# Transformer block on one core: attention scores from exactly split q and k in three one-pass products, and P V after every two key tiles

## The chip, the cores and the metric

The kernel runs on one core of a Trainium2 chip. The metric is the device time of one execution in microseconds, as the median over runs. All work of an engine is queued in the order in which the program issues it: TensorE (PE, with its weight loads PEld), VectorE (DVE), ScalarE (ACT), GpSimd (POOL), and SyncE (SP), which here issues all the DMAs.

## The reference

One pre-norm block on x of 2 x 2048 x 256 in float32: attention with a compressed key/value (rank 64) and a compressed query (rank 128), 16 heads, then a gated feed-forward part with weights given as whole numbers. A head's q and k have 48 numbers: 16 of content and 32 with rotary position (rope). Cut to what matters here:

```python
q = jnp.concatenate([q_content, q_rope], axis=-1)      # (2, 16, 2048, 16 + 32)
k = jnp.concatenate([k_content, k_rope], axis=-1)
scores = jnp.einsum('bhqd,bhkd->bhqk', q, k) * scale
scores = jnp.where(causal[None, None], scores, -inf)
attn = jax.nn.softmax(scores, axis=-1)
out = jnp.einsum('bhqk,bhkd->bhqd', attn, v)
x = x + out.transpose(0, 2, 1, 3).reshape(Bx, Tx, 256) @ W_o
x = x + ffn(layernorm(x))
```

## The kernel before

**First stage.** The sequence is cut into chunks of 512 tokens, four for each batch, eight in all. For each chunk the kernel normalizes, transposes and projects, applies rope, and stores q and k, head by head and transposed, in DRAM (`qr`, `kr` for the rope rows, `qc_d`, `kc` for the content rows). V stays in SBUF. From the fifth chunk on, `load_first` puts the first pieces of the attention stage between the projections: four k loads, two q loads, two empty places, and `from_first` for the first step.

**Attention.** A step is a batch b, a group u of four heads and a chunk g of 512 queries; there are 32, with g running fastest. It goes over the key chunks c = 0 to g. A key chunk has four key tiles of 128; in the last one (c = g, the diagonal chunk) tile j has only the queries from 128 j on, so products are 512, 384, 256 and 128 wide. Four heads stand as two pairs r and two row halves a: the 48 rows of a head lie at partitions 0 to 47 or 64 to 111, so two heads' products (one for each half) use different rows of the PE array. For each key tile and pair r, `scores` makes two float32 products into one PSUM tile of two banks (three such tiles, `ps_big`), ACT takes exp of both banks at once into an `es` tile (12 of them), and in the diagonal chunk POOL clears what lies above the diagonal. `values` multiplies by V: four heads use 32 columns of the array each and add into one PSUM tile `acc`. At the end of a step `gather` copies `acc` (ACT) and stores it (`ad`).

The order is written out by hand and kept for all five engines. All four tiles of a key chunk are scored, then the first tile of the next chunk, and only then comes P V of the finished chunk:

```python
for k, job in enumerate(jobs):
    job()
    if k == 0 and waiting:
        waiting.pop()()
    if c == 0 and k == 1 and i + 1 < len(steps):
        from_first(*steps[i + 1])
```

`load_q` brings a step's q two steps ahead, `load_k` its k four steps ahead, each with four DMAs (two of rope rows, two of content rows). `from_first` (L142) subtracts the first key from all keys, which changes no softmax.

**Other work in the attention stage.** `loads` also stores V, loads and converts the feed-forward weights, and for the first batch's chunks calls in turn `packed` (gathers a chunk's attention output and sums), `inverted` (1/sum, sent round through DRAM into `rb`) and `divided`. Near the end, `early` starts the output projection and layer norm of the first two chunks.

**Feed-forward part.** Its matmuls already work on fp32r halves ("hi" and "lo") of their inputs: `gu` (L722) and `d` (L750).

Of the kernel before, what the change touches and what calls it, by code (L numbers as in the profile page):

```python
# [30 lines left out]
AHEAD = 2  # L31
LN_EPS = 1e-5
RMS_EPS = 1e-6
NEG = -3.0e38
# [6 lines left out]
def block_kernel(ctx: ExitStack, tc: tile.TileContext, x, w_kv, g_kv, w_kc, w_v, w_q, w_qh, w_kr, w_o,  # L41
# [14 lines left out]
    qpool = qkv.enter_context(tc.tile_pool(name="qpool", side="right", bufs=AHEAD + 1))  # L56

    ident = const.tile([P, P], FP, tag="ident", name="ident")
    make_identity(nc, ident)
# [64 lines left out]
    kT, qT = {}, {}  # L124
    k_tiles = [kpool.tile([P, 2, CH], FP, tag=f"kT_{i}", name=f"kT_{i}") for i in range(2 * NC)]
    k0 = {}

    def load_k(b, u, g):
        kT[b, u, g] = t = k_tiles[u % 2 * NC + g]
        load_heads(t, kr[b, g], kc[b, g][:, :HD, :], u)  # L130

    def from_first(b, u, g):


        t = kT[b, u, g]
        if g == 0:
            k0[b, u] = small.tile([P, 2], FP, tag="k0", name=f"k0_{b}_{u}")
        for a in range(2):
            rows = slice(64 * a, 64 * a + DIM)
            if g == 0:  # L140
                nc.vector.tensor_copy(k0[b, u][rows], t[rows, :, 0])
            nc.vector.tensor_tensor(t[rows], t[rows], k0[b, u][rows].unsqueeze(2).to_broadcast([DIM, 2, CH]),  # L142
                                    ALU.subtract)

    def load_q(b, u, g):
        qT[b, u, g] = t = qpool.tile([P, 2, CH], FP, tag="qT", name=f"qT_{b}_{u}_{g}")
        load_heads(t, qr[b, g], qc_d[b, g], u)

    written = ExitStack()

# [1 line left out]
    with ExitStack() as actx:  # L152
# [204 lines left out]
        def job(i, k):  # L357
            if i < len(chunks):
                chains[i][k]()
# [21 lines left out]
        for d in range(2):  # L381
            rope_columns(w_kr_sb[:, d, :], w_kr_raw[d])

        first_loads = ([(load_k, step) for step in steps[:NC]] + [(load_q, step) for step in steps[:AHEAD]]
                       + 2 * [(lambda *step: None, steps[0])] + [(from_first, steps[0])])

        def load_first(i):
            if i >= NC and first_loads:
# [3 lines left out]
        for i, one in enumerate(chunks):  # L392
# [35 lines left out]
            if i == 0:  # L428
                for to in kc.values():
                    nc.sync.dma_start(out=to[:, HD, :], in_=ones)  # L430

    fw = ctx.enter_context(tc.tile_pool(name="fw", bufs=1))
    apool = ctx.enter_context(tc.tile_pool(name="apool", bufs=4))
# [24 lines left out]
    def inverted(b, g):  # L458

        n = f"{b}_{g}"  # L460
        rec = small.tile([P, 64], FP, tag="rec", name=f"rec_{n}")
        nc.vector.reciprocal(rec, parts_of[b, g])  # L462
        rd = dram.tile([NH, CH], FP, tag="rd", bufs=4, name=f"rd_{n}")
        nc.sync.dma_start(out=rd.rearrange("h (j i) -> (h j) i", i=64), in_=rec)
        parts_of[b, g] = rb = apool.tile([P, 2, CH], FP, tag="rb", bufs=2, name=f"rb_{n}")
# [65 lines left out]


    with ExitStack() as actx:
        espool = actx.enter_context(tc.tile_pool(name="espool", side="right", bufs=12))
# [5 lines left out]
        def exp_jobs(b, u, g):  # L540

            n = f"{b}_{u}_{g}"
            es = {}
            last_kt = NT * (g + 1) - 1

            def first(kt):
                c, j = divmod(kt, NT)
                return c, j, j * P if c == g else 0

            def scores(kt, p):  # L550

                c, j, off = first(kt)
                pairs = (0, 1) if off >= CH // 2 else (p,)

                def job():
                    if p not in pairs[:1]:
                        return
                    w = CH - off
                    ps = big(f"st_{n}_{kt}_{p}")
                    e = espool.tile([P, 2, CH], FP, tag="es", name=f"es_{n}_{kt}_{p}")  # L560
                    for i, r in enumerate(pairs):
                        for a in range(2):
                            rows = slice(64 * a, 64 * a + DIM)
                            nc.tensor.matmul(ps[:, a, i * w:(i + 1) * w],  # L564
                                             lhsT=kT[b, u, c][rows, r, j * P:(j + 1) * P],
                                             rhs=qT[b, u, g][rows, r, off:], start=True, stop=True)
                        es[kt, r] = e[:, :, i * w:(i + 1) * w]
                    used = len(pairs) * w
                    nc.scalar.activation(e[:, :, :used], ps[:, :, :used], AF.Exp, scale=SCALE)  # L569
                    if c == g:  # L570
                        if len(pairs) == 1:
                            block, pattern = e[:, :, :P], [[0, 2], [1, P]]
                        else:
                            block = e[:, :, :used].rearrange("k a (r q) -> k a r q", r=2)[:, :, :, :P]
                            pattern = [[0, 2], [0, 2], [1, P]]
                        nc.gpsimd.affine_select(out=block, in_=block, compare_op=ALU.is_ge, fill=0.0, base=0,  # L576
                                                pattern=pattern, channel_multiplier=-1)
                return job

            def values(*kts):  # L580
                def job():
                    if kts[0] == 0:
                        acc[b, u, g] = ps_acc.tile([P, CH], FP, tag="acc", name=f"acc_{n}")
                    for kt in kts:
                        c, j, off = first(kt)
                        for p in range(2):
                            for a in range(2):
                                h = 4 * u + 2 * p + a
                                r0 = 32 * (2 * p + a)
                                nc.tensor.matmul(acc[b, u, g][r0:r0 + 32, off:],  # L590
                                                 lhsT=vv[b, c][:, j, h * VW:h * VW + 32],
                                                 rhs=es[kt, p][:, a], start=(kt == 0), stop=(kt == last_kt),
                                                 tile_position=(0, r0))
                return job

            def gather():
                at = fin.tile([P, CH], FP, tag="at", name=f"at_{n}")
                nc.scalar.copy(at, acc[b, u, g])  # L598
                nc.sync.dma_start(out=ad[b, g][4 * u:4 * u + 4].rearrange("h e f -> (h e) f"), in_=at)

            jobs = []
            for c in range(g + 1):
                kts = range(c * NT, (c + 1) * NT)
                job = values(*kts)
                if c == g:
                    job = lambda job=job: (job(), gather())
                jobs.append(([(lambda kt=kt: (scores(kt, 0)(), scores(kt, 1)())) for kt in kts], job))
            return jobs

        def loads(i):  # L610

            if i + AHEAD < len(steps):
                load_q(*steps[i + AHEAD])
            if i + NC < len(steps):
                load_k(*steps[i + NC])
            if i == NU * NC + 6:
                x1[0, 0] = load_x(xpool, 0, 0)
                x1[0, 1] = load_x(spare, 0, 1)
# [2 lines left out]
                nc.sync.dma_start(out=vd[one], in_=vv[one])  # L621

            j, k = divmod(i - (NU * NC + 2), 3)
            if 0 <= j < 3 or (j, k) == (3, 0):
# [7 lines left out]
        def whole(src, shape, name, n):  # L632
# [16 lines left out]
            for i in range(2):  # L649
# [15 lines left out]
        waiting = []  # L665
        for i, step in enumerate(steps):
            loads(i)
            by_chunk = exp_jobs(*step)
            for c, (jobs, values) in enumerate(by_chunk):
                for k, job in enumerate(jobs):  # L670
                    job()
                    if k == 0 and waiting:
                        waiting.pop()()
                    if c == 0 and k == 1 and i + 1 < len(steps):
                        from_first(*steps[i + 1])
                    if k in (0, 2):
                        for one, g in early.get((i, c, k), ()):
                            one(*groups[g])
                waiting.append(values)
        waiting.pop()()  # L680

    qkv.close()

# [308 lines left out]
```

## Time and profile before

| | |
|---|---|
| median of 3 runs | 1084.23 us (1083.06 to 1085.67) |
| the profiled execution | 1085.72 us, span 1083.9 us |
| granted TensorE clock | 0.997 |
| PE, ACT, DVE, POOL busy over the span | 98%, 60%, 29%, 26% |
| scores L564: matmul records, busy | 2560, 495.6 us |
| P V L590: matmul records, busy | 2560, 251.5 us |
| exp L569: instructions, busy | 576, 512.9 us |
| first stage, attention, feed-forward | to about 167 us, to about 915 us, to the end |

Busy times of matmuls include the time in which results drain, and matmuls overlap, so the step from one matmul's start to the next one's says more than its duration. A program's float32 product appears as two matmul records and two weight loads. The chain of work that ended last names, for each stretch of time, the engine that the end of the span depended on.

### The profile page before, as it was taken

The page shows a single profiled execution, that of the slowest core. Times are in us where ns is not written, and L with a number is a line of the kernel's source. Part 1 is how long each engine was busy: PE and PEld are TensorE (multiplying, and loading weights), DVE is VectorE, ACT ScalarE, POOL GpSimd, SP SyncE. Part 2 cuts the span into 40 slices and gives each one's busy share as a digit, 9 for nine tenths or more (in the row PEclk, how much of TensorE's full clock was granted, in tenths as well). Part 3 has the DMA queues.
Part 4 walks back from the last instruction along what each step waited for, and adds up shares of the span by engine and source line. Part 5 has one row for each costly group of instructions (what it writes and reads, how often), then busy time and mean ns, then how long its engine had stood idle before and what let it go on. Part 6 is the DMA issues. An engine that isn't in the chain of part 4 may idle for free.

```text
span 1083.9 us, 16862 instructions
## 1 busy us (share of the span) xinstructions
PE 1066.2 (98%) x6687; PEld 536.8 (50%) x6687; DVE 309.8 (29%) x454; ACT 653.9 (60%) x817; POOL 282.0 (26%) x379
## 2 busy tenths in 40 slices
PE   8899999999999999999999999999999999999997
PEld 5455554444443443434344344443435344889886
DVE  5577776000310220230001212004001210556552
ACT  3243336777776776777777767767766766343242
POOL 4566756002110200211111021021101111445353
PEclk9999999999999999999999999999999999999999
DMA  7746746112410421311131133132201000342201
GB/s 180 238 162 216 251 162 201 40 40 78 135 61 1 145 68 61 94 54 40 37 103 39 31 99 99 40 81 79 60 5 45 11 10 20 126 124 63 80 20 43
DMA packets 54457, 93.27 MB, mean 86 GB/s; under 512 B 9312, under 2 KB 23008, under 8 KB 54368
## 3 DMA queue, kind: packets, MB, share of 16 engines
q1 hardware_dynamic: 54368, 92.09, 27.6%
q8 instruction: 55, 0.90, 0.4%
q14 instruction: 34, 0.28, 0.1%
HBM read 49.09 MB, written 42.98 MB: 85 GB/s over the span
## 4 chain that ended last, share of the span: by engine, by line
PE 82%; DVE 1%; POOL 0%; ACT 0%; issue 0%; DVEq 0%; ACTq 0%
PE st L564 45%; PE acc L590 22%; PE gu L722 8%; PE d L750 4%; PE ps_o L485 3%; PE tp_f L528 1%; POOL es L576 0%; DVE h L729 0%; DVE small_ones L696 0%; DVE x_f_lo L530 0%; POOL rstd_f L69 0%; POOL rstd_f L70 0%; ACT es L569 0%; ACT x_f_hi L529 0%; DVE y L757 0%
## 5 line engine op out<-in xcount | busy, mean ns | idle before, releaser
L569 ACT ACTIVATE es<-st 128x1024 f32<-128x1024 f32 (+1 forms) x576 | 512.9, 993 | 170.0 <-PE st L564 168.2
L564 PE MATMUL st<-qT,kT 48*128 48x512 f32 (+3 forms) x2560 | 495.6, 536 | 1.7 <-ACT v_sb L348 1.2
L564 PEld LDWEIGHTS st<-qT,kT 48*128 48x128 f32 x2560 | 226.0, 186 | 250.8 <-ACT es L569 119.7
L576 POOL TENSOR_SCALAR_AFFINE_SELECT es<-es 128x256 f32<-128x256 f32 (+1 forms) x192 | 97.4, 516 | 641.1 <-ACT es L569 641.1
L590 PE MATMUL acc<-es,v_sb 128*32 128x512 f32 (+3 forms) x2560 | 251.5, 531 | 0.7 <-POOL es L576 0.7
L590 PEld LDWEIGHTS acc<-es,v_sb 128*32 128x32 f32 x2560 | 74.6, 109 | 185.4 <-issue 145.9
L142 DVE TENSOR_TENSOR kT<-kT,k 48x1024 f32<-48x1024 f32 x64 | 82.4, 1287 | 20.7 <-DMA kT<-kc 18.2
L725 ACT ACTIVATE silu<-gu 128x512 f32<-128x512 f32 x48 | 28.6, 599 | 92.9 <-PE gu L722 92.9
L734 POOL TENSOR_TENSOR hT_lo<-h,hT_hi 128x512 fp32r<-128x512 f32 x48 | 61.8, 1289 | 81.8 <-ACT hT_hi L733 74.7
L304 PE MATMUL rp_k<-xln,w_kr_sb 128*128 128x512 f32 x128 | 58.1, 598 | 0.0
L729 DVE SCALAR_TENSOR_TENSOR h<-gu,silu 128x512 f32<-128x512 f32 x48 | 33.0, 690 | 77.9 <-ACT silu L725 51.2
L462 DVE RECIPROCAL rec<-all_sums 128x64 f32<-128x64 f32 x8 | 4.4, 548 | 160.4 <-DMA all_sums<-ad 160.4
L750 PE MATMUL d<-w_d,hT_lo 128*128 128x256 f32 x192 | 46.4, 283 | 0.0
L750 PE MATMUL d<-w_d,hT_hi 128*128 128x256 f32 x192 | 46.4, 283 | 0.0
L598 ACT COPY at<-acc 128x512 f32<-128x512 f32 x32 | 18.8, 586 | 40.5 <-PE acc L590 38.1
L722 PE MATMUL gu<-x_f_hi,w_g 128*128 128x512 f32 x96 | 39.4, 411 | 0.2 <-DVE h L729 0.2
L491 DVE TENSOR_TENSOR x<-ps_o,x 128x1024 f32<-128x1024 f32 x8 | 9.8, 1225 | 101.2 <-PE ps_o L485 99.7
L722 PE MATMUL gu<-x_f_lo,w_g 128*128 128x512 f32 x96 | 37.5, 391 | 0.0
L722 PE MATMUL gu<-x_f_lo,w_u 128*128 128x512 f32 x96 | 37.4, 390 | 0.0
L722 PE MATMUL gu<-x_f_hi,w_u 128*128 128x512 f32 x96 | 37.4, 390 | 0.0
L750 PEld LDWEIGHTS d<-w_d,hT_lo 128*128 128x128 f32 x192 | 36.8, 192 | 0.3
L750 PEld LDWEIGHTS d<-w_d,hT_hi 128*128 128x128 f32 x192 | 36.8, 192 | 0.3
(99 smaller groups left out, 764.7 us busy)
## 6 DMA issues: line engine op xcount, KB each, us to landing
kr<-tcos_k SPq DMA_DIRECT2D x16, 512.0 KB
qr<-tcos_q SPq DMA_DIRECT2D x16, 512.0 KB
kT<-kr SPq DMA_DIRECT2D x64, 128.0 KB
qT<-qr SPq DMA_DIRECT2D x64, 128.0 KB
ad<-at SPq DMA_DIRECT2D x32, 256.0 KB
x<-in_x_dram SPq DMA_DIRECT2D x15, 512.0 KB
vd<-v_sb SPq DMA_DIRECT2D x8, 574.0 KB
qc<-cont_q SPq DMA_DIRECT2D x8, 512.0 KB
```

The source lines that it names most:

```text
L142: nc.vector.tensor_tensor(t[rows], t[rows], k0[b, u][rows].unsqueeze(2).to_broadcast([DIM, 2, CH]), ALU.subtract)
L304: nc.tensor.matmul(ps[:, s, :], lhsT=w_kr_sb[:, d, cols], rhs=xln[b, g][:, d, :], start=(d == 0), stop=(d == 1))
L485: nc.tensor.matmul(ps[:, t * C:(t + 1) * C], lhsT=attn[b, g][:, d, t * P:(t + 1) * P], rhs=w_o_sb[:, d, :], start=(d == 0), stop=(d == 1))
L564: nc.tensor.matmul(ps[:, a, i * w:(i + 1) * w], lhsT=kT[b, u, c][rows, r, j * P:(j + 1) * P], rhs=qT[b, u, g][rows, r, off:], start=True, ...
L569: nc.scalar.activation(e[:, :, :used], ps[:, :, :used], AF.Exp, scale=SCALE)
L576: nc.gpsimd.affine_select(out=block, in_=block, compare_op=ALU.is_ge, fill=0.0, base=0, pattern=pattern, channel_multiplier=-1)
L590: nc.tensor.matmul(acc[b, u, g][r0:r0 + 32, off:], lhsT=vv[b, c][:, j, h * VW:h * VW + 32], rhs=es[kt, p][:, a], start=(kt == 0), stop=(kt ...
L722: nc.tensor.matmul(ps[:, k, :], lhsT=w[:, d, cols], rhs=x2[b, g][s][:, d, :], start=(d == 0 and s == 0), stop=(d == 1 and s == 1))
L725: nc.scalar.activation(s, ps[:, 0, :], AF.Silu, scale=WS)
L729: nc.vector.scalar_tensor_tensor(h, ps[:, 1, :], WS, s, ALU.mult, ALU.mult)
L734: nc.gpsimd.tensor_tensor(lo, h, hi.bitcast(FP), ALU.subtract)
L750: nc.tensor.matmul(ps[t], lhsT=parts[b, g][s][:, f, t * P:(t + 1) * P], rhs=w_d[:, f, :], start=(f == 0 and s == 0), stop=(f == NF - 1 and ...
```

## The change

- **Split.** k (after the first key is subtracted) and q are split into a high part, rounded to fp32r, and the rest. k has four copies of a head's content and two of its rope rows in 64 rows; the constant `lows` marks the rows in which the low part is to stand. `split_k` and `split_q` do this on DVE, through a shared tile `rest`.
- **Three products.** Each score group adds three fp32r products with 64 rows into the same PSUM tile: rope rows (both parts of k) with q's low part, rope rows with q's high part, and content rows (all four combinations).
- **Loads.** k is loaded in 12 DMAs (four rope, eight content) and q likewise, both two steps ahead; there are five k sets and three q sets. A table `plan` says after which key tile each load and split is issued.
- **Order.** Outside the diagonal chunk P V is issued for two key tiles at a time, two tiles later. The diagonal chunk's P V still comes after the next step's first tile; the copy of `acc` now comes one tile after that.
- **Buffers.** es 12 to 8, `attn` 4 to 3, `rb` 2 to 1; `packed(0, 3)` moves from step 27 to step 30.
- **First loads.** `load_first` now issues k and q of the first two steps and the four splits of the first step.

```diff
-    def from_first(b, u, g):
-        t = kT[b, u, g]
...
-            nc.vector.tensor_tensor(t[rows], t[rows], k0[b, u][rows].unsqueeze(2).to_broadcast([DIM, 2, CH]),
-                                    ALU.subtract)
+    def load_rope(t, ropes, u):
+        src = ropes[4 * u:4 * u + 4].rearrange("(p a) r s f -> a (r s) p f", a=2)
+        for a in range(2):
+            for i in range(2):
+                nc.sync.dma_start(out=t[64 * a + RD * i:64 * a + RD * i + RD], in_=src[a])
+    def load_content(t, contents, u):
+        src = contents[4 * u:4 * u + 4, :HD, :].rearrange("(p a) r f -> a r p f", a=2)
+        for a in range(2):
+            for i in range(4):
+                nc.sync.dma_start(out=t[64 * a + HD * i:64 * a + HD * i + HD], in_=src[a])
...
+    def split_k(b, u, g, i):
+        t = k_of(b, u, g)[i]
...
+        firsts = k0[b, u, i]
+        for p in range(2):
+            nc.vector.tensor_scalar(rest[:, p], t[:, p], firsts[:, p:p + 1], lows[:, i:i + 1], ALU.subtract, ALU.mult)
+        for p in range(2):
+            nc.vector.scalar_tensor_tensor(t[:, p].bitcast(FR), t[:, p], firsts[:, p:p + 1], rest[:, p].bitcast(FP),
+                                           ALU.subtract, ALU.subtract)
+    def split_q(b, u, g, i):
+        t, other, content = q_of(b, u, g)
+        if i:
+            nc.vector.tensor_scalar(rest, content, lows[:, 2:3], None, ALU.mult)
+            nc.vector.tensor_tensor(content.bitcast(FR), content, rest.bitcast(FP), ALU.subtract)
+        else:
+            nc.vector.tensor_scalar(other.bitcast(FR), t, lows[:, 0:1], None, ALU.mult)
+            nc.vector.tensor_tensor(other.bitcast(FR), t, other, ALU.subtract)
+            nc.vector.tensor_tensor(t.bitcast(FR), t, other, ALU.subtract)
...
-        first_loads = ([(load_k, step) for step in steps[:NC]] + [(load_q, step) for step in steps[:AHEAD]]
-                       + 2 * [(lambda *step: None, steps[0])] + [(from_first, steps[0])])
+        first_loads = ([(of, (*step, i)) for step in steps[:2] for of in (load_k, load_q) for i in range(2)]
+                       + [(of, (*steps[0], i)) for of in (split_k, split_q) for i in range(2)])
...
+                    k, q = k_of(b, u, c), q_of(b, u, g)
+                    products = ((k[0], q[1]), (k[0], q[0]), (k[1], q[2]))
                     for i, r in enumerate(pairs):
-                        for a in range(2):
-                            rows = slice(64 * a, 64 * a + DIM)
-                            nc.tensor.matmul(ps[:, a, i * w:(i + 1) * w],
-                                             lhsT=kT[b, u, c][rows, r, j * P:(j + 1) * P],
-                                             rhs=qT[b, u, g][rows, r, off:], start=True, stop=True)
+                        for n_of, (kp, qp) in enumerate(products):
+                            for a in range(2):
+                                rows = slice(64 * a, 64 * a + 64)
+                                nc.tensor.matmul(ps[:, a, i * w:(i + 1) * w],
+                                                 lhsT=kp[rows, r, j * P:(j + 1) * P].bitcast(FR),
+                                                 rhs=qp[rows, r, off:].bitcast(FR),
+                                                 start=(n_of == 0), stop=(n_of == len(products) - 1))
...
+        plan = {
+            (0, 0): ((load_k, 2), (load_q, 2)),
+            (1, 0): ((split_k, 0), (load_q, 2)), (1, 1): ((load_k, 2),), (1, 2): ((split_q, 1),),
+            (2, 0): ((split_k, 0),), (2, 1): ((split_q, 1),), (2, 2): ((load_q, 2),), (2, 3): ((load_k, 2),),
+            (3, 0): ((split_k, 0), (load_q, 2)), (3, 1): (), (3, 2): ((split_k, 1),), (3, 3): ((split_q, 1),),
+            (3, 4): ((load_k, 2),), (3, 5): ((split_q, 2),)}
+        due = []
         for i, step in enumerate(steps):
...
+            for n, (c, k, job) in enumerate(jobs):
+                job()
+                for one in due:
+                    one[0] -= 1
+                while due and due[0][0] <= 0:
+                    due.pop(0)[1]()
+                group.append(n)
+                if c == step[2]:
+                    if k == NT - 1:
+                        due.append([1, lambda of=values(*group), gather=gather:
+                                    (of(), due.insert(0, [1, gather]))])
+                        group = []
+                elif k % 2:
+                    due.append([2, values(*group)])
+                    group = []
```

More of the change, by code (lines that the diff above doesn't have):

```diff
@@ L30 @@
 ROWS = DIM + 1
-AHEAD = 2
 LN_EPS = 1e-5
@@ L55, in block_kernel @@
     kpool = qkv.enter_context(tc.tile_pool(name="kpool", side="right", bufs=1))
-    qpool = qkv.enter_context(tc.tile_pool(name="qpool", side="right", bufs=AHEAD + 1))
     ident = const.tile([P, P], FP, tag="ident", name="ident")
@@ L123, in block_kernel @@
     steps = [(b, u, g) for b in range(B) for u in range(NU) for g in range(NC)]
[L124 to L130, printed above, removed]
-    def from_first(b, u, g):
-        t = kT[b, u, g]
-        if g == 0:
-            k0[b, u] = small.tile([P, 2], FP, tag="k0", name=f"k0_{b}_{u}")
-        for a in range(2):
-            rows = slice(64 * a, 64 * a + DIM)
-            if g == 0:
-                nc.vector.tensor_copy(k0[b, u][rows], t[rows, :, 0])
-            nc.vector.tensor_tensor(t[rows], t[rows], k0[b, u][rows].unsqueeze(2).to_broadcast([DIM, 2, CH]),
-                                    ALU.subtract)
@@ L145, in load_q, with place_sets @@
-    def load_q(b, u, g):
-        qT[b, u, g] = t = qpool.tile([P, 2, CH], FP, tag="qT", name=f"qT_{b}_{u}_{g}")
-        load_heads(t, qr[b, g], qc_d[b, g], u)
+    k_sets, q_sets, k0 = [], [], {}
+    def place_sets(pool, ks, qs):
+        for n in range(len(k_sets), ks):
+            k_sets.append([pool.tile([P, 2, CH], FP, tag=f"k{i}_{n}", name=f"k{i}_{n}") for i in range(2)])
+        for n in range(len(q_sets), qs):
+            q_sets.append([pool.tile([P, 2, CH], FP, tag=f"q{i}_{n}", name=f"q{i}_{n}") for i in range(3)])
@@ new lines, in block_kernel @@
+    place_sets(kpool, 2, 2)
+    rest = kpool.tile([P, 2, CH], FR, tag="rest", name="rest")
+    lows = const.tile([P, 3], FP, tag="lows", name="lows")
+    for i, of in enumerate((ident.rearrange("p (b h c) -> p b h c", h=2, c=RD)[:, :, 1, :],
+                            ident.rearrange("p (b h c) -> p b h c", h=2, c=HD)[:, :, 1, :],
+                            ident.rearrange("p (b c) -> p b c", c=64)[:, :, HD:3 * HD])):
+        nc.vector.tensor_reduce(lows[:, i:i + 1], of, AX.XY, ALU.add)
@@ new lines, in k_of, with q_of @@
+    def k_of(b, u, g):
+        return k_sets[((b * NU + u) * NC + g) % 5]
+    def q_of(b, u, g):
+        return q_sets[((b * NU + u) * NC + g) % 3]
+    def load_rope(t, ropes, u):
[8 more added lines that the diff above has]
+                nc.sync.dma_start(out=t[64 * a + HD * i:64 * a + HD * i + HD], in_=src[a])
@@ new lines, in load_k, with load_q @@
+    def load_k(b, u, g, i):
+        t = k_of(b, u, g)[i]
+        if i:
+            load_content(t, kc[b, g], u)
+        else:
+            load_rope(t, kr[b, g], u)
+    def load_q(b, u, g, i):
+        t = q_of(b, u, g)[2 * i]
+        if i:
+            load_content(t, qc_d[b, g], u)
+        else:
+            load_rope(t, qr[b, g], u)
+    def split_k(b, u, g, i):
+        t = k_of(b, u, g)[i]
+        if g == 0:
+            k0[b, u, i] = small.tile([P, 2], FP, tag=f"k0_{i}", name=f"k0_{i}_{b}_{u}")
+            nc.vector.tensor_copy(k0[b, u, i], t[:, :, 0])
+        firsts = k0[b, u, i]
[4 more added lines that the diff above has]
+                                           ALU.subtract, ALU.subtract)
@@ new lines, in split_q @@
+    def split_q(b, u, g, i):
+        t, other, content = q_of(b, u, g)
+        if i:
+            nc.vector.tensor_scalar(rest, content, lows[:, 2:3], None, ALU.mult)
+            nc.vector.tensor_tensor(content.bitcast(FR), content, rest.bitcast(FP), ALU.subtract)
+        else:
+            nc.vector.tensor_scalar(other.bitcast(FR), t, lows[:, 0:1], None, ALU.mult)
+            nc.vector.tensor_tensor(other.bitcast(FR), t, other, ALU.subtract)
+            nc.vector.tensor_tensor(t.bitcast(FR), t, other, ALU.subtract)
@@ L430, in block_kernel @@
                     nc.sync.dma_start(out=to[:, HD, :], in_=ones)
+    place_sets(qkv.enter_context(tc.tile_pool(name="kpool1", side="right", bufs=1)), 5, 3)
     fw = ctx.enter_context(tc.tile_pool(name="fw", bufs=1))
-    apool = ctx.enter_context(tc.tile_pool(name="apool", bufs=4))
+    apool = ctx.enter_context(tc.tile_pool(name="apool", bufs=3))
     ps_big = ctx.enter_context(tc.tile_pool(name="ps_big", bufs=3, space=PSUM))
@@ L464, in inverted @@
         nc.sync.dma_start(out=rd.rearrange("h (j i) -> (h j) i", i=64), in_=rec)
-        parts_of[b, g] = rb = apool.tile([P, 2, CH], FP, tag="rb", bufs=2, name=f"rb_{n}")
+        parts_of[b, g] = rb = apool.tile([P, 2, CH], FP, tag="rb", bufs=1, name=f"rb_{n}")
         for d in range(2):
@@ L533, in block_kernel @@
     with ExitStack() as actx:
-        espool = actx.enter_context(tc.tile_pool(name="espool", side="right", bufs=12))
+        espool = actx.enter_context(tc.tile_pool(name="espool", side="right", bufs=8))
         fin = actx.enter_context(tc.tile_pool(name="fin", side="right", bufs=2))
@@ L560, in job @@
                     e = espool.tile([P, 2, CH], FP, tag="es", name=f"es_{n}_{kt}_{p}")
+                    k, q = k_of(b, u, c), q_of(b, u, g)
+                    products = ((k[0], q[1]), (k[0], q[0]), (k[1], q[2]))
                     for i, r in enumerate(pairs):
-                        for a in range(2):
-                            rows = slice(64 * a, 64 * a + DIM)
-                            nc.tensor.matmul(ps[:, a, i * w:(i + 1) * w],
-                                             lhsT=kT[b, u, c][rows, r, j * P:(j + 1) * P],
-                                             rhs=qT[b, u, g][rows, r, off:], start=True, stop=True)
+                        for n_of, (kp, qp) in enumerate(products):
[5 more added lines that the diff above has]
+                                                 start=(n_of == 0), stop=(n_of == len(products) - 1))
                         es[kt, r] = e[:, :, i * w:(i + 1) * w]
@@ L602, in exp_jobs @@
             for c in range(g + 1):
[L603 to L608, printed above, removed]
+                for k in range(NT):
+                    kt = c * NT + k
+                    jobs.append((c, k, lambda kt=kt: (scores(kt, 0)(), scores(kt, 1)())))
+            return jobs, values, gather
         def loads(i):
[L612 to L615, printed above, removed]
             if i == NU * NC + 6:
@@ L623, in loads @@
             j, k = divmod(i - (NU * NC + 2), 3)
-            if 0 <= j < 3 or (j, k) == (3, 0):
+            if i == len(steps) - 2:
+                packed(0, 3)
+            if 0 <= j < 3:
                 (packed, inverted, divided)[k](0, j)
@@ L664, in block_kernel @@
                  (end, 1, 2): ((normed, 1),)}
-        waiting = []
+        plan = {
[4 more added lines that the diff above has]
+            (3, 4): ((load_k, 2),), (3, 5): ((split_q, 2),)}
@@ L666, in block_kernel @@
+        due = []
         for i, step in enumerate(steps):
             loads(i)
[L668 to L679, printed above, removed]
@@ L680, in block_kernel @@
-        waiting.pop()()
+            jobs, values, gather = exp_jobs(*step)
+            group = []
[13 more added lines that the diff above has]
+                    due.append([2, values(*group)])
+                    group = []
+                if i == 0 and k % 2 == 0:
+                    split_q(*steps[1], k // 2)
+                if k % 2 == 0:
+                    for of, ahead in plan.get((step[2], c * 2 + k // 2), ()):
+                        if i + ahead < len(steps):
+                            for part in range(2):
+                                of(*steps[i + ahead], part)
+                if k in (0, 2):
+                    for one, g in early.get((i, c, k), ()):
+                        one(*groups[g])
@@ L682, in block_kernel @@
+        while due:
+            due.pop(0)[1]()
     qkv.close()
```

## The prediction

> **What bounds the kernel now.** I read the busy shares first, then the chain of work that ended last, then the matmul groups, then the timeline around one chunk of attention. The page says:
>
> ```profile
> PE 1066.2 (98%) x6687; PEld 536.8 (50%) x6687; DVE 309.8 (29%) x454; ACT 653.9 (60%) x817; POOL 282.0 (26%) x379
> PE 82%; DVE 1%; POOL 0%; ACT 0%; issue 0%; DVEq 0%; ACTq 0%
> ```
>
> TensorE (PE) is busy throughout and alone makes the chain; ACT is second. The chain in order of time shows the attention stage as a strict alternation of scores (st) and P V (acc), here a full chunk of four key tiles and a diagonal chunk:
>
> ```profile
> 603.84 7.07 PE st L564 x32
> 610.91 3.57 PE acc L590 x32
> ...
> 625.12 4.68 PE st L564 x32
> 629.80 2.29 PE acc L590 x32
> ```
>
> A full chunk costs 7.07 + 3.57 = 10.64 us, a diagonal one 4.67 + 2.29 = 6.96 us. There are 8 (batch, head group) pairs with 6 full and 4 diagonal chunks each: 48 x 10.64 + 32 x 6.96 = 733 us, the stretch from 167 to 900 us. So PE's sequence explains attention to a per cent. Inside one burst (timeline):
>
> ```profile
> 603.77 7.14 PE L564 MATMUL st<-qT,kT 48*128 48x512 f32 x32
> 604.31 0.19 PEld L564 LDWEIGHTS st<-qT,kT 48*128 48x128 f32 x2 [0.23 <-issue]
> 604.74 0.19 PEld L564 LDWEIGHTS st<-qT,kT 48*128 48x128 f32 x2 [0.23 <-issue]
> 605.01 7.44 ACT L569 ACTIVATE es<-st 128x1024 f32<-128x1024 f32 x8 [3.19 <-PE st L564]
> 607.91 0.45 PEld L564 LDWEIGHTS st<-qT,kT 48*128 48x128 f32 x4 [0.41 <-ACT es L569]
> 608.83 0.39 PEld L564 LDWEIGHTS st<-qT,kT 48*128 48x128 f32 x4 [0.47 <-ACT es L569]
> ```
>
> The two row halves load weights together (two loads in one 0.19 us) and run together. Each float32 product is recorded as two matmuls; a pair of halves therefore takes 2 x 0.43 us for 512 columns. The eight exps run at 7.44 / 8 = 0.93 us, and late in the burst the loads already wait for them, 0.92 us apart. ACT is thus only 7% slower than the score burst feeds it; it recovers during P V. That is what a faster score burst will meet.
>
> **What a one-pass product costs.** The feed-forward part already has one-pass (fp32r) matmuls with changing weights:
>
> ```profile
> 1000.07 0.28 PE L750 MATMUL d<-w_d,hT_lo 128*128 128x256 f32 x1
> 1000.19 0.28 PE L750 MATMUL d<-w_d,hT_hi 128*128 128x256 f32 x1
> ...
> 1007.47 0.40 PE L722 MATMUL gu<-x_f_hi,w_g 128*128 128x512 f32 x1
> 1007.70 0.40 PE L722 MATMUL gu<-x_f_lo,w_g 128*128 128x512 f32 x1
> ```
>
> Start to start this is 0.120 us for 256 columns and 0.227 us for 512 (7.27 us for 32 in the chain). For 384 I take 0.173 between them. For 128 no one-pass row exists; below it is half of 0.120, above it 0.120. The nearest rows are those where the 128-column weight load sets the pace (kvq: 16 loads in 1.86 us, 0.111 each), so 0.116. No fp32r matmul on 64 rows is in the trace. Either two halves overlap, as the float32 halves do here, or they do not; I take the first. Per slot the lower end is 0.215 us (half of 0.43), the upper 0.240.
>
> The Trainium skill ("TensorE: Matmul & The Clock Gate", LDWEIGHTS) gives a load as columns over 1.2 GHz, 107 ns for 128 columns. If the two halves' loads had to queue, a slot would never be under 0.213 us by that figure, and the diagonal chunks would be some 44 us dearer in all (an estimate from that page). The two loads within one 0.19 us above speak against queueing.
>
> **PE's own sum.** Scores go from one float32 product (two recorded matmuls) to three one-pass ones: 2560 matmuls become 3840. P V keeps its 2560. A full chunk has 8 score pairs, so 24 slots: 24 x 0.227 = 5.45 us. A switch costs 7.07 - 16 x 0.43 = 0.19 us into scores and 3.57 - 8 x 0.43 = 0.13 us into P V; with two key tiles at a time both are paid twice per full chunk. So 5.45 + 0.38 + 3.44 + 0.26 = 9.53 us against 10.64, or -1.11 x 48 = -53 us. A diagonal chunk has six slots of each width, 6 x (0.227 + 0.173 + 0.120 + 0.116) + 0.19 = 4.01 us against 4.67, or -0.66 x 32 = -21 us. Together -74 us.
>
> **What is late next: exp and the three PSUM buffers.** From a group's last matmul to its exp the timeline gives about 0.27 us (0.2 to 0.3); an exp starts 0.92 us after the one before, its record lasts 1.045, and the next weight load in that buffer needs about 0.15 more: 1.20 us from exp start to refill. A score group is now 3 x 0.227 = 0.68 us. After a step's first tile and the diagonal P V, the order runs three tiles (six groups) in a row. Group 0 is done at 0.19 + 0.68 = 0.87, its exp runs from 1.14, its buffer is free at 2.34; group 3 wants it at 2.23: 0.11 late. The exps then follow each other at 0.92: group 4 waits 0.24, and group 5 another 0.24 plus 0.59, since the copy of acc (L598, 586 ns) now stands in ACT's queue after that step's second tile. That is 1.18 us per step, x 32 = 38 us. The ordinary two-tile bursts pay the 0.11 alone, 72 times, 8 us. Together +46 us. Ends: nothing, if refill is quicker, and 58 us, with the latencies at their upper values. Everything on PE behind a blocked score load (the P V of earlier tiles too) waits with it. The 12 to 8 es buffers cost nothing: two groups of two tiles are exactly eight, and P V frees the first four before the next exp.
>
> **DVE, DMA and the start.** Removed per step: two subtractions of 1287 ns (82.4 us in all). Added per step: four tensor_scalar and four scalar_tensor_tensor of 128x512, two tensor_scalar and three tensor_tensor of 128x1024. With L142's 1.24 us back to back, L729's 0.69 for the 512-wide form, and the L87 rows (345 ns apart for 256 columns in the feed-forward part, scaled by columns: 0.61 and 1.15) that is 5.2 + 6.0 = 11.2 us, 358 us over 32 steps. Attention lasts some 705 us, DVE's other work there is 24 us, and each split stands a good part of a step ahead of its use, so it is hidden. The upper end: L87 in the first stage takes 835 ns apart, beside POOL's work; then a step's splits take 19 us and the 17 us steps of two chunks would show a few us each, 8 times.
>
> Loads: a step issues 24 DMAs (2 MB) instead of 8 (0.77 MB). Their queue SP needs 0.43 to 0.47 us each when free, 11 us of a step of 22 on average; DMA was 21% busy in attention. The queue's wait for a free q set is met at each step's start, and behind it stands only the store of acc. Hidden.
>
> In the first stage (167 us, PE 159 busy) there are 48 instead of 24 first loads, at 0.43 to 1.4 us of SP each; rope stores stand behind them, whose buffers DVE and then PE need. SP idles about a third between 100 and 140 us, so 0 to 12, taken 3 us. DVE does 13 us of splitting there where it did 5, with 5 us idle until the last tiles: 3 us. Together +6. The move of one group's gathering DMAs, one buffer less for attn and rb, and the mask sums are under other waits: each rb is divided before the next is asked for. The feed-forward part is unchanged.
>
> **Sum.** -74 + 46 + 6 = -22 us on the span of 1083.9. The profiled execution took 1085.72 us, 1.8 more than its span and 1.5 more than the median of 1084.23; so 1062 us at the median.
>
> **Rivals.**
> - *PE cannot start instructions fast enough (slower).* Weight loads and matmuls of attention rise from 10240 to 12800. The d run above starts 96 in 5.75 us, 60 ns each. If 60 ns were PE's limit over long runs, attention took 768 us instead of 733: with the +6, +41, about 1125 us. It decides from 57 ns. Against: kvq ran 32 in 1.86 us (58) and two diagonal chunks in a row 256 in 13.9 us (54), neither certainly at a limit. Chance 0.12. The same skill page names 62 ns of sequencer time per matmul in one decode setting; two per slot would be 124 ns, and only the narrow slots would grow, by 2 us in all (estimate); no run here shows that setting.
> - *No PSUM stalls (much faster).* The refill is quick enough or ACT runs closer to the matmuls: -74 + 6, about 1016; with half the stall 1039. Chance 0.16 for 1016 to 1039.
> - *Splitting and loading show up (slower).* If the slow L87 rate holds in attention and SP holds up the first stage: 12 + 8 x 4 + 10 more on DVE's sharing, against the 28 left: about 1110. Chance 0.08.
> - *Halves of 64 rows do not overlap:* every slot doubles, over 300 us slower. Chance 0.04.
> - *The gain is just eaten:* stalls of 58 and slots of 0.235 leave the time unchanged. Chance 0.04.
>
> **Numbers.** The forecast has 0.56, with its own range 1042 to 1078 (slots 0.215 to 0.240, first stage 0 to 12). Faster 0.56 + 0.16 = 0.72, same 0.04, slower 0.24; a measurement of this kernel can tell 0.2% (2 us). The range 1022 to 1112 takes in the third rival and leaves out the serial halves (0.04), the instruction limit (0.12) and the last quarter of the stall-free case (0.04).
>
> **What would show it.** Right: st slots of about 0.23 us per pair with two loads at once; full chunks near 9.6 to 10 us; score loads waiting for ACT es several tens of us in all, most in the three-tile bursts; ACT in attention above 70%. Wrong: st matmuls twice as long apart; PE idle or slow with no releaser (issue); waits on DVE's k and q tiles inside steps; a first stage over 180 us.

## The result and the profile after

The changed kernel takes 1064.44 us (1063.71 to 1064.98), against 1083.64 us for the kernel before: a ratio of 0.982 (95% interval 0.9803 to 0.9836). The forecast was 1062, with a range of 1042 to 1078. The profiled execution took 1064.98 us, its span 1063.2. The engine line and the chain shares, from the page of the kernel after:

```profile
PE 1030.7 (97%) x7967; PEld 619.9 (58%) x7967; DVE 557.8 (52%) x809; ACT 652.8 (61%) x817; POOL 324.5 (31%) x379
PE 79%; ACT 7%; issue 4%; DVE 4%; DMA 3%; SPq 2%; POOL 1%; DVEq 0%; ACTq 0%; POOLq 0%
```

PE is still busy nearly throughout. Its two chain shares, 82% before and 79% here, can't be compared: the chain of before is followed back only to 170 us, where attention starts, and PE has nearly all of it from there; this one goes back to the start. What can be compared is ACT: it had no share and now has 7%, nearly all of it through L628 (exp) and L657 (the copy of `acc`), which run only in attention. DVE went from 309.8 to 557.8 us of work.

Attention, from the start of the first score matmul to the start of the last of P V, went from 745.2 us (170.3 to 915.5) to 723.0 us (171.9 to 895.0). The feed-forward tail behind it kept its length, 168.4 and 168.2 us. So the whole result lies in attention. The chain in order of time shows two ordinary two-tile rounds, and then the end of a step (columns: start, length, what; `...` stands for lines left out):

```profile
248.22 3.04 PE st L622 x24
251.26 1.85 PE acc L649 x16
253.11 3.04 PE st L622 x24
256.15 1.85 PE acc L649 x16
...
262.76 3.06 PE st L622 x36
265.82 2.29 PE acc L649 x32
```

A round is 4.89 us, so a full chunk is 9.78 instead of 10.64 us. The x36 burst holds two narrow diagonal tiles and the next step's first tile: 36 matmuls and 36 weight loads in 3.06 us, followed by 32 and 32 in 2.29 us. And this is a three-tile burst, from the end of a diagonal P V to the next P V:

```profile
228.92 2.29 PE acc L649 x32
231.21 0.91 PE st L622 x6
...
232.20 0.65 ACT es L628
...
233.12 0.42 ACT es L628
233.54 0.49 issue
234.03 0.27 ACT at L657
...
234.49 1.06 ACT es L628
...
235.60 0.96 PE st L622 x6
236.57 1.85 PE acc L649 x16
```

Here the chain leaves PE: a score group waits for a PSUM buffer, which waits for an exp, and that exp for the copy of `acc` (`at L657`). ACT's own timeline shows why the wait is this long:

```profile
232.20 1.94 ACT L628 ACTIVATE es<-st 128x1024 f32<-128x1024 f32 x2 [1.98 <-PE st L622]
234.03 0.59 ACT L657 COPY at<-acc 128x512 f32<-128x512 f32 x1
234.49 3.81 ACT L628 ACTIVATE es<-st 128x1024 f32<-128x1024 f32 x4
```

ACT sat idle for 1.98 us, did two exps, and then put the copy of acc, whose input had been ready since 231.21, in front of the exps that PE was waiting for.

For the experiments I use one more measure: the **cycle**, the time of four steps (one batch and head group), from one g = 3 copy of acc to the next in the trace. A trace has seven; the first six are free of the first stage and of the feed-forward work that starts in the last steps. Before, the six took 91.7 to 91.9 us, after 88.3 to 89.0 us. Below I give the value without disturbances, at or near the low end: 91.7 us before, 88.3 us after.

### The profile page after: what moved, and what is told of

Its sections match the earlier page's. It is cut to its first block, busy times and chain, and to the rows that moved or that the text cites. A ratio compares the mean times of both kernels' runs of the same rounds, so it can differ in the third digit from the quotient of the medians.

```text
span 1063.2 us, 20992 instructions
## 1 busy us (share of the span) xinstructions
PE 1030.7 (97%) x7967; PEld 619.9 (58%) x7967; DVE 557.8 (52%) x809; ACT 652.8 (61%) x817; POOL 324.5 (31%) x379
## 4 chain that ended last, share of the span: by engine, by line
PE 79%; ACT 7%; issue 4%; DVE 4%; DMA 3%; SPq 2%; POOL 1%; DVEq 0%; ACTq 0%; POOLq 0%
PE st L622 31%; PE acc L649 23%; PE gu L800 8%; ACT es L628 6%; PE d L828 4%; PE rp_k L358 3%; PE ps_o L540 3%; PE rp_q L361 1%; PE kvq L312 1%; PE kvq L315 1%; SPq L163 1%; SPq L156 1%; DMA q<-qc 1%; ACT at L657 1%; PE cp_q L379 1%
## 5 line engine op out<-in xcount | busy, mean ns | idle before, releaser
L628 ACT ACTIVATE es<-st 128x1024 f32<-128x1024 f32 (+1 forms) x576 | 519.4, 990 | 191.1 <-PE st L622 191.1
L622 PE MATMUL st<-q,k 64*128 64x512 f32 (+3 forms) x3840 | 454.0, 377 | 17.5 <-ACT es L628 12.8
L622 PEld LDWEIGHTS st<-q,k 64*128 64x128 f32 x3840 | 312.3, 185 | 193.1 <-ACT es L628 142.8
L635 POOL TENSOR_SCALAR_AFFINE_SELECT es<-es 128x256 f32<-128x256 f32 (+1 forms) x192 | 140.2, 744 | 575.2 <-ACT es L628 574.4
L649 PE MATMUL acc<-es,v_sb 128*32 128x512 f32 (+3 forms) x2560 | 262.5, 536 | 0.2
L199 DVE TENSOR_SCALAR q<-q,lows 128x1024 fp32r<-128x1024 f32 x32 | 25.4, 794 | 144.3 <-DMA q<-qr 143.2
L190 DVE SCALAR_TENSOR_TENSOR k<-k,k,rest 128x512 fp32r<-128x512 f32 x128 | 92.5, 763 | 0.0
L188 DVE TENSOR_SCALAR rest<-k,k,lows 128x512 fp32r<-128x512 f32 x128 | 69.3, 583 | 14.4 <-DMA k<-kr 9.7
L197 DVE TENSOR_TENSOR q<-q,rest 128x1024 fp32r<-128x1024 f32 x32 | 42.3, 1321 | 3.1
L201 DVE TENSOR_TENSOR q<-q,q 128x1024 fp32r<-128x1024 f32 x32 | 41.6, 1300 | 3.4 <-DVE q L200 0.5
L200 DVE TENSOR_TENSOR q<-q,q 128x1024 fp32r<-128x1024 f32 x32 | 42.5, 1330 | 1.1
L358 PEld LDWEIGHTS rp_k<-xln,w_kr_sb 128*128 128x128 f32 x128 | 23.8, 194 | 29.6 <-issue 29.4
```

The costliest lines, as they stand in the source:

```text
L188: nc.vector.tensor_scalar(rest[:, p], t[:, p], firsts[:, p:p + 1], lows[:, i:i + 1], ALU.subtract, ALU.mult)
L190: nc.vector.scalar_tensor_tensor(t[:, p].bitcast(FR), t[:, p], firsts[:, p:p + 1], rest[:, p].bitcast(FP), ALU.subtract, ALU.subtract)
L197: nc.vector.tensor_tensor(content.bitcast(FR), content, rest.bitcast(FP), ALU.subtract)
L200: nc.vector.tensor_tensor(other.bitcast(FR), t, other, ALU.subtract)
L358: nc.tensor.matmul(ps[:, s, :], lhsT=w_kr_sb[:, d, cols], rhs=xln[b, g][:, d, :], start=(d == 0), stop=(d == 1))
L622: nc.tensor.matmul(ps[:, a, i * w:(i + 1) * w], lhsT=kp[rows, r, j * P:(j + 1) * P].bitcast(FR), rhs=qp[rows, r, off:].bitcast(FR), start= ...
```

## The experiments

All are edits to the changed kernel, unless said otherwise. Each is told with its ratio to the kernel before; after is 0.982.

**The copy of acc directly after the diagonal P V.**

```diff
-                        due.append([1, lambda of=values(*group), gather=gather:
-                                    (of(), due.insert(0, [1, gather]))])
+                        due.append([1, lambda of=values(*group), gather=gather: (of(), gather())])
```

> Theory (the gain left on PE is eaten by score groups that wait for exp to free one of three PSUM buffers, most of it in the three-tile burst after a step's diagonal P V, where the 0.59 us copy of acc stands between two tiles' exps in ACT's queue): the copy directly after the diagonal P V runs while ACT has nothing else to do, so the last group of the burst starts 0.59 us earlier, 32 times: about 18 us less, 1046 us, and a four-step cycle of 86.2 us where it was 88.3. Rival (three buffers and the pace of exp alone make the stalls, the place of the copy is hidden): within 3 us of 1064.

Measured: 1048.87 us, ratio 0.9672 (0.9647 to 0.9697); the cycle is 86.4 us. The copy now runs in ACT's idle time (ACT timeline), and the three-tile burst takes 4.88 us where it took 5.36 (chain):

```profile
445.65 0.59 ACT L657 COPY at<-acc 128x512 f32<-128x512 f32 x1 [1.03 <-PE acc L649]
446.57 5.61 ACT L628 ACTIVATE es<-st 128x1024 f32<-128x1024 f32 x6 [0.34 <-PE st L622]
```

```profile
443.29 2.29 PE acc L649 x32
445.58 4.88 PE st L622 x33
450.46 1.85 PE acc L649 x16
```

The rival, that the place of the copy is hidden, falls. One ACT instruction of 0.59 us in the wrong place of a queue cost 15.6 us, where the whole change had brought 19.2.

**P V one tile later instead of two** (with the copy as above).

```diff
-                    due.append([2, values(*group)])
+                    due.append([1, values(*group)])
```

> With the copy directly after the diagonal P V, and P V of two full tiles one tile later instead of two, so that no burst has six full groups in a row. Theory (stalls come from long bursts): another 11 us less than with the copy alone, 1035 us, a cycle of 84.8 us. Rival (the two-tile delay is what hides exp from P V): P V waits for the exps of the tile just scored, loads of acc show waits on ACT es, and the time is back at 1046 or above.

Measured: 1042.15 us, ratio 0.9608 (0.9581 to 0.9636), cycle 85.1 us. The cycle came as expected (84.8), the total fell by 7 us instead of 11; the last cycle, with the feed-forward work in it, got nothing (94.3 and 94.6 us). No burst has three full tiles any more. Score loads' waits, from the list of waits (us in total, times, longest), of after, of the copy alone and of this kernel:

```profile
PEld st L622 <- ACT es L628: 142.8, 266, 0.9
```

```profile
PEld st L622 <- ACT es L628: 127.0, 259, 0.8
```

```profile
PEld st L622 <- ACT es L628: 24.3, 100, 0.8
PEld st L622 <- issue: 85.0, 127, 0.8
```

This list is no measure of the time lost. The first edit took 16 us off the span and 16 us off the line for ACT; the second took 8 us off the span and 103 us off that line, but 78 us of them came back on the line for "issue", idle time before a load for which the profile shows no releaser (85.0 us here, 7.2 with the copy alone, 7.0 in after). Both lines together fell by 25 us, still three times what the span did.

**Two products instead of three.**

```diff
-                    products = ((k[0], q[1]), (k[0], q[0]), (k[1], q[2]))
+                    products = ((k[0], q[0]), (k[1], q[2]))
```

> Leaves out the product of the rope rows with q's low part: 2560 score matmuls instead of 3840. PE's own sum falls by 640 slots, 48 x 8 x 0.227 + 32 x 2 x 0.636 = 128 us. Theory (exp and its three buffers are already late next): the stalls rise from about 47 to 120 us, the time falls by 57 us only, to about 1008 us, a cycle of 81.5 us. Rival (PE's own sequence still sets the end, the waits of score loads are slack): it falls by over 110 us, to about 950 us.

The list of products under "The change" and the expectation name this product wrongly. By `split_q`, each of q's two rope tiles holds the high part in 32 of its 64 rows and the low part in the other 32, and so does k. The product left out adds high x high and low x low, the other one the two mixed terms. So this kernel lacks the main part of the rope scores, and only its time is of use.

Measured: 1012.43 us, ratio 0.9335 (0.9295 to 0.9376), cycle 81.9 us (the six took 81.3 to 83.1). A third of the score matmuls, 128 us of PE's own sum, is worth 52 us. The chain now alternates between PE and ACT in every two-tile round:

```profile
406.79 1.85 PE acc L649 x16
408.64 0.68 PE st L622 x4
409.36 0.04 issue
409.41 1.04 ACT es L628
410.44 0.04 issue
410.49 0.73 PE st L622 x4
411.22 1.85 PE acc L649 x16
```

The rival (PE's sequence alone sets the end) falls. With three PSUM buffers, exp is next behind PE in the two-tile rounds too, not only in the long bursts. It is not alone: POOL's selects have 4% of this run's chain (ACT 15%), where they had 1% in after, so a part of the 76 us that did not come is likely theirs.

**The kernel before, with the new order of P V alone.** The scores stay float32; the loop over `due` replaces that over `waiting`, with `from_first` where it was:

```diff
...
-                waiting.append(values)
...
+                elif k % 2:
+                    due.append([2, values(*group)])
+                    group = []
```

> The kernel before with only the order of P V (and of the copy of acc) changed as in the change: float32 products, P V after every two full tiles, two tiles later. Theory (every switch between scores and P V costs 0.33 us, and the copy behind the second tile costs 0.59 us of stall per step also here): 48 x 0.33 = 16 us from switches and about 14 us from stalls, some 1114 us, a cycle of 95.5 us where it was 91.7. Rival (switches overlap with waits that are there anyway): within 6 us of 1084.

Measured: 1109.26 us, ratio 1.0227 (1.0202 to 1.0252), cycle 95.1 us. So this part of the change, taken alone, costs 2.3%. A score burst of two full tiles takes 3.63 us (3.44 for eight slots of 0.43, and 0.19), P V 1.85; the last line is from a three-tile burst:

```profile
422.13 3.63 PE st L564 x16
425.76 1.85 PE acc L590 x16
```

```profile
417.57 0.59 ACT at L598
```

Two rounds are 10.96 us against 10.64 for one of four tiles: 0.32 us per added switch, as taken (0.33). That makes 1.9 of the 3.4 us per cycle; for the rest the late copy (`at L598`) is the likely cause, since the chain goes through it, but it was not moved here.

**Rounding without splitting.** k and q get one DVE instruction per tile (shown for q's rope rows):

```diff
             nc.vector.tensor_scalar(other.bitcast(FR), t, lows[:, 0:1], None, ALU.mult)
-            nc.vector.tensor_tensor(other.bitcast(FR), t, other, ALU.subtract)
-            nc.vector.tensor_tensor(t.bitcast(FR), t, other, ALU.subtract)
+            nc.vector.tensor_scalar(t.bitcast(FR), t, lows[:, 0:1], None, ALU.mult)
```

> Leaves out the splitting: k and q are rounded with one DVE instruction for each tile (four tensor_scalar of 128x512, three of 128x1024 per step), and no low parts are made; loads, products and order are those of the change. DVE's added work falls from some 11 to some 5 us per step. Theory (splitting is hidden, except in the first three steps, where PE waited for split q): the cycle stays at 88.3 us within 0.5, the waits of the first steps shrink, 1060 us. Rival (splitting costs all along, through POOL's selects, which went from 507 to 730 ns beside it, or through late k and q tiles): the cycle falls by 1 us or more, 1055 us or less.

Measured: 4082.02 us in all. By its code this kernel adds every score twice: the two rope tiles of q become the same (rounded, in the rows that `lows` marks), and of the four copies of the content rows two are kept. The kernel ends with a second computation that runs when a sum of exp exceeds 2^24 (`GROWN`) or a feed-forward weight is too large. With the same weights it ran here, from about 1058 us on, and in no other run; doubled scores are the likely reason. The expected totals therefore can't be compared; attention, which lies before it, can. The cycle is 88.3 us, as in after. So in the steady state the split costs nothing, though DVE was busy 154 us here (170 to 890 us) and 337 in after (175 to 885 us).

What it does cost lies at the start. In the first stage PE waits 2.0 us for DVE (`rp_k <- DVE tsin_q`) in after and not here, and the first g = 3 copy comes at 263.6 us here and at 270.3 in after, though attention starts only 0.9 us earlier (171.0 and 171.9 us). And POOL's select of 128x256 took 446 ns before, 678 in after, 478 here:

```profile
L576 POOL TENSOR_SCALAR_AFFINE_SELECT es<-es 128x256 f32<-128x256 f32 x128 | 56.9, 446 | 622.1 <-ACT es L569 622.1
```

```profile
L635 POOL TENSOR_SCALAR_AFFINE_SELECT es<-es 128x256 f32<-128x256 f32 x128 | 85.7, 678 | 537.9 <-ACT es L628 537.4
```

```profile
L630 POOL TENSOR_SCALAR_AFFINE_SELECT es<-es 128x256 f32<-128x256 f32 x128 | 61.0, 478 | 554.2 <-ACT es L623 553.6
```

**The third step's q loaded ahead of its k.**

```diff
+                        if i == 0:
+                            of = {load_k: load_q, load_q: load_k}[of]
                         if i + ahead < len(steps):
```

> Only in the first step, the loads of the third step's q are issued ahead of those of its k, which is needed later. In the change the third step's first scores waited for that q (loads of 0.42 us each in SP's queue behind the k loads, then the split), and the first four steps took 5 us more against before than the later ones. Theory (that queue order is the start-up loss): 3 to 5 us less, about 1060 us, no PE wait on DVE q near 196 us. Rival (the loads start late for another reason, a buffer of the first stage that comes free late or DVE being busy): within 1 us of 1064.

In after, PE stood still before the third step's scores, and the P V behind them was slow; here neither is so (PE timelines of after and of this kernel):

```profile
196.18 0.57 PE L622 MATMUL st<-q,k 64*128 64x512 f32 x2 [0.55 <-DVE q L201]
198.79 1.35 PE L622 MATMUL st<-q,k 64*128 64x512 f32 x8 [2.04 <-DVE q L197]
200.07 4.05 PE L649 MATMUL acc<-es,v_sb 128*32 128x512 f32 x32
```

```profile
193.87 3.12 PE L622 MATMUL st<-q,k 64*128 64x256 f32 x36
196.92 2.36 PE L649 MATMUL acc<-es,v_sb 128*32 128x512 f32 x32
```

Measured: 1062.38 us, ratio 0.9807 (0.9794 to 0.9821). The wait is gone, and the first g = 3 copy comes 4.8 us earlier (at 265.5 us instead of 270.3). The span fell by 3.6 us, the median by 2 us, less than expected, and the intervals of the two ratios overlap. That the order removes the wait is shown by the trace; that the total gains is likely, not proven.

Two things go beyond the theory. The slow P V is the granted clock: it was 0.57 between 200 and 204 us in after and 1.00 in this kernel, and the same 32 matmuls took 4.05 and 2.36 us. So 1.7 us of the loss came as a low clock after the wait, not as the wait. And the queue order alone does not make the wait: plain rounding has the old order and no such wait. There the loads began 2.1 us earlier, and the rope rows of this q were rounded within 1.6 us of their start on DVE (189.8 us); in after the five split instructions ran from 192.7 to 198.7 us. So late loads and 6 us of splitting made the wait together.

**All three together.** 

> The copy of acc directly after the diagonal P V, P V of two full tiles one tile later, and the third step's q loaded ahead of its k. If the start-up loss and the exp stalls are separate: the 1042 us of the first two together less the gain of the third, 1038 us. If the start-up wait only moves to another tile: 1042 us.

Measured: 1038.09 us, ratio 0.9581 (0.9567 to 0.9596), cycle 85.1 us. The expected 1038 came. The interval touches that of the first two edits (0.9581 to 0.9636), so that the third edit adds its part is likely, not proven. This beats both kernels: the change's gain of 1.8% becomes 4.2% by order alone.

Not tried: the new products with P V every four tiles as before. It needs ten es tiles (eight of the finished chunk and two of the next tile), where the change has eight.

## Why the prediction was right, point by point

- **One-pass slots.** Taken 0.227, 0.173, 0.120 and 0.116 us for 512, 384, 256 and 128 columns, halves overlapping. From start to start in the trace of after (200 to 800 us, medians) the pairs follow each other in 0.231, 0.175, 0.117 and, less sharply, about 0.11 us, with the two halves 3 to 4 ns apart. No 64-row fp32r row was in the trace before; the step from the 128-row rows and the float32 halves held.
- **PE's own sum, and the stalls.** Predicted: -74 us from slots and switches, +46 us from exp and its three buffers, -28 us. The 733 us for before were right as a sum (eight cycles of 91.7 are 734), but not as "the stretch from 167 to 900 us": attention ran from 170.3 to 915.5 us, with feed-forward matmuls and waits between its last steps. Scaled to eight, the measured cycle of 88.3 us is 706 us; PE's own sum was 733 - 74 = 659. So the stalls are 47 us, if the own sum is right. The burst worked out by hand (0.19 + 6 x 0.68 + 1.18 = 5.45 us) took 5.36. There are 24 such bursts and not 32: in the eight steps with g = 0 only the narrow tiles and the next step's first tile follow there, and that burst took 4.76 us where its slots and switch add up to 4.01. The two kinds lose some 31 us together where 38 were predicted; the rest is in shorter bursts (8 predicted). The copy moved and a product left out show that exp, its buffers and the place of the copy make these stalls. With the copy moved and P V one tile later, 85.1 x 8 - 659 = 22 us are still there, and nothing was tried on them.
- **The copy of acc** was priced at 0.59 us per step, 19 us in all; moving it brought 15.6 us.
- **Splitting.** Taken 358 us on DVE, hidden; the new groups add up to 342 us of busy time. Mistakes cancel in part: tensor_scalar of 1024 columns took 0.79 and 0.89 us, not 1.15, but scalar_tensor_tensor 0.76, not 0.69, and tensor_tensor 1.30 to 1.33, not 1.24. It is hidden in the steady state, as shown.
- **The step that failed: the start.** I put +6 us on the first stage and nothing on the first steps of attention. The first stage ended 1.6 us later than before (171.9 against 170.3 us), but the profile of before had a 3.3 us PE wait (ktp on ACT kvn) that neither after has nor the run with the old products, which keeps the first stage of before and starts attention at 167.0 us. Against that run the change cost 4.9 us: 2.0 by DVE, and likely some 1.4 by the granted clock, which was 0.83 between 150 and 160 us in after and 1.00 in the run of all three, whose first stage is the same and ended at 170.5 us. And "each split stands a good part of a step ahead of its use" is wrong for the second and third step: PE waited 0.8 us (178 us) and 2.6 us (196 to 199 us) for split q, the third step's behind 12 k loads in SP's queue, and 1.7 us went with the low clock behind that wait. That is the 5 us by which the first four steps gained less than the later ones. The total held partly by luck: the start cost some 10 us (4.9 + 5) where +6 was put, and only the early wait in the profile of before brought the two near each other (1.6 + 5).
- **The rivals.** An instruction limit of 57 ns or more: the x36 burst and the x32 P V behind it hold 136 matmuls and loads in 5.35 us, 39 ns each, and the wider slots are as taken. It fell. A stall-free kernel near 1016 us fell with the chain through ACT. Serial halves fell with the slot of 0.231 us, and queued loads of two halves with the narrow slots of about 0.12 us. The rival of DVE and loads showed only at the start.

## What to carry to other kernels

When the engine that sets the end gets faster work, price its new waits before its gain: here 74 us of PE time became 27 in the steady state, because the next engine was already 7% slower than the old burst and only three buffers stood between them. That price can be worked out by hand from three durations (one producer group, one consumer step, the time from consumer start to refill) for the longest burst in the program order. Then look at what else stands in the consumer's queue: one 0.59 us copy, issued a tile too late, cost about 15 us, while ACT had stood idle for 1.98 us just before its exps.

## What the runs showed of the hardware that was not expected

POOL's select slowed from 446 to 678 ns beside the splitting on DVE and went back to 478 ns without it. In the trace of after, the 65 of the 128 selects of 128x256 during which DVE ran nothing took 401 to 408 ns; the 14 that overlapped L200 and L201 alone, the tensor_tensor instructions with two inputs in SBUF, took 914 to 1383 ns. The Trainium skill ("SBUF — State Buffer", Who interferes with whom) has it that DVE and GpSimd share a port pair, and that a DVE instruction with two SBUF inputs contends with a GpSimd instruction that reads SBUF, as one in a two-port mode does. The trace agrees for two inputs. In plain rounding, where the added DVE instructions have one tensor input, selects beside them still took up to 967 ns; whether that is a two-port mode was not told apart.

In one step of after, four selects (two of them of 128x512) took 5.22 us beside the splitting:

```profile
269.59 1.23 DVE L200 TENSOR_TENSOR q<-q,q 128x1024 fp32r<-128x1024 f32 x1
269.82 5.22 POOL L635 TENSOR_SCALAR_AFFINE_SELECT es<-es 128x256 f32<-128x256 f32 x4 [2.16 <-ACT es L628]
270.92 1.24 DVE L201 TENSOR_TENSOR q<-q,q 128x1024 fp32r<-128x1024 f32 x1
```

That cycle took 88.95 us against 88.3 for the least disturbed, so it cost PE at most 0.6 us there.

Going between scores, on two row halves, and P V, on four column groups, adds 0.32 us for both ways (two rounds of 10.96 us against one of 10.64; the prediction splits it into 0.19 and 0.13). What this time is spent on is not shown. Paid 48 more times, it cost the new order some 15 us, which the float32 kernel could not earn back.
